# Memory read of layer 3: scores of two token tiles by seven half-size products, and rows weighted on another engine

## The chip, the core and the metric

The kernel runs on one core of a Trainium2 chip. The metric is the device time of one execution in microseconds; smaller is better. The profile names the engines PE (matrix products, TensorE), PEld (its weight loads), DVE (VectorE), ACT (ScalarE), POOL (GpSimd) and SP (SyncE, which here only issues transfers). Each engine takes its instructions strictly in the order of its own queue and waits there until what an instruction needs is ready.

## The reference, cut to what matters

The program is a chain of four layers on an image batch `x` of 4 x 512 channels x 32 x 32 positions, in 32-bit floating point. Layers 0 and 2 are attention layers, layer 1 is a gating layer. The change is nearly all in layer 3, a read of a memory of 2048 items of 512 numbers:

```python
q = jnp.transpose(x, (0, 2, 3, 1)).reshape(-1, C)   # x is group-normalized here; 4096 tokens x 512
att = q @ mempool.T                                 # 4096 x 2048 scores
vals, idx = jax.lax.top_k(att, k)                   # k = 8
vals = jax.nn.softmax(vals, axis=1)
att_sparse = jnp.zeros_like(att).at[rows, idx].set(vals)
out = att_sparse @ mempool                          # 8 weighted rows of the memory per token
```

The result is added to `x`.

## The kernel before, in words

The main path is `fast_net`; a general version of the network behind a flag is compiled in but not run on these inputs. The layers follow each other image by image (`b` from 0 to 3), with T = 1024 tokens and C = 512 channels for each image, KC = 4 blocks of P = 128 channels. In layers 0 to 2 many products of two matrices are done already by a scheme of seven half-size products (`seven`, with its sums made by `add7` and `sub7` on DVE, line 1050).

Layer 3 works on tiles of 128 tokens, 8 to an image, 32 in all (`tiles`). The normalized image is `xn3[b]`, the transposed memory is `memT`, four pieces of 128 x 2048, two of them in a buffer of their own and two in the large buffer `eT`. Nearly every instruction of this stage is put in by `pin`, so that each engine's order is the order in which the code issues them. For each tile:

- `attention` (lines 1514 to 1531) makes the 128 x 2048 scores: two halves of 1024, each in one of three PSUM places `pair` (two banks each, taken in turn by `next_pair`), each half by 8 products of 128 x 512 (line 1523), 16 products to a tile. ACT copies each half into a place `att` in SBUF (line 1528). There are three such places.
- `pick` (from line 1533) finds on DVE the eight largest scores of each token (MAX8, line 1543) and their positions (FIND_INDEX8, line 1545). POOL then issues eight indirect transfers that fetch the eight memory rows of each token into `got` (line 1548; three places). DVE makes the negated maximum (line 1554), ACT the exponentials and their sum (line 1557). SP loads the tile of `x` to be added to (line 1560).
- `read` (from line 1588) scales the weights (lines 1565 and 1566) and adds up the eight weighted rows on DVE: one product by a scalar (line 1593) and seven multiply-and-adds (line 1595). PE turns the result back to channels by tokens (line 1600) into one of two PSUM banks, `pv` and `pt`.
- `put` adds it to `x` on DVE (line 1605) and SP stores it (line 1606).

The loop at the end of `fast_net` runs over steps `s`: scores of tile s, pick of tile s-1, put of tile s-3, read of tile s-2. The last two tiles are read differently: `diagonals` (line 1572, ACT) makes diagonal matrices of the weights and `read_last` (line 1581, PE) multiplies the fetched rows by them, 32 products to a tile. Beside this, `prepare3` loads and normalizes the next image on ACT, and `behind` is a generator whose steps finish the statistics of the last image.

Just ahead of layer 3 stands the output product of layer 2's last image, `put_out2` (lines 1468 to 1488): four blocks of 16 products, each evicted by DVE in two adds, with an ACT scaling of a piece of `x` ahead of each add, and statistics behind. The scores of tile 0 stand ahead of it.

In layer 0 the gate of layer 1 is made by a generator, `gating`, whose steps ("links") are issued one at a time between other work: small products on PE, small operations on POOL, DVE and ACT. `go_on` issues the next link. At the border between two images of layer 0 `go_on` is called in each of four steps, and then once behind each product of `seven_keys` (or of `seven_by_channels` at the last border).

Of the kernel before, what the change touches and what calls it, by code (L numbers as in the profile page):

```python
# [16 lines left out]
P = 128  # L17
B = 4
# [23 lines left out]
def fast_net(ctx: ExitStack, tc: tile.TileContext, a: dict, out: bass.AP, flag: bass.AP):  # L42
# [147 lines left out]
    def tokens(src):  # L190
        return lambda k, n: src[:, k, n * NB:(n + 1) * NB]
# [56 lines left out]
    def big(tag, name):  # L248

        return apool.tile([P, KC, T], F32, tag=tag, name=name)  # L250
# [3 lines left out]
    def eight_k(shape, name, at=None):  # L254

        if at is None:
            at = turns8[0] % 3
            turns8[0] += 1
        return apool.tile(shape, F32, tag=f"w{at}", name=name)
# [1205 lines left out]
        nc.vector.tensor_mul(  # L1465
            I["o"][:, m, n * NB:(n + 1) * NB], I.pop(("pv", m, n)), I.pop(("rb", m, n)))

    def put_out2(b):
        I = img[b]
        s1 = l2[b][1]  # L1470
        mv = small.tile([P, KC, 2], F32, tag="mv", name=f"mv_d{b}")

        def add_out(m, ps):
            st = small.tile([P, 2, 6], F32, tag="bnst", name=f"st_d{b}_{m}")
            for n in range(T // NB):
                xr = apool.tile([P, NB], F32, tag="xr", bufs=2, name=f"xr_c{b}_{m}_{n}")
                nc.sync.dma_start(out=xr, in_=x1[b][:, m, n * NB:(n + 1) * NB])
                pin(nc.scalar.activation(
                    xr, xr, AF.Identity, bias=I["tb"][:, m:m + 1], scale=s1[:, m:m + 1]))
                nc.vector.tensor_add(xr, ps[:, n * NB:(n + 1) * NB], xr)  # L1480
                nc.sync.dma_start(out=x2[b][:, m, n * NB:(n + 1) * NB], in_=xr)
                nc.vector.bn_stats(st[:, n, :], xr)
            nc.vector.bn_aggr(mv[:, m, :], st.rearrange("p i s -> p (i s)"))

        for m in range(KC):
            project(I["Wp"], tokens(I["o"]), m, None, lambda ps: add_out(m, ps), f"p2_{b}")
        gc3 = const.tile([P, 2, KC], F32, tag=f"gc3_{b}", name=f"gc3_{b}")
        l3[b] = (mv, gc3)

# [21 lines left out]
            ))  # L1511
            yield

    def attention(b, tt, between=None):

        nm = f"{b}_{tt}"
        att = eight_k([P, NI], f"att_{nm}")
        for i, (lo, hi) in enumerate(
                ((0, T), (T, T + NB), (T + NB, NI)) if (b, tt) == tiles[-1] else ((0, T), (T, NI))):
            sc = flat2(next_pair())  # L1520
            for i0 in range(lo, hi, NB):
                for k in range(KC):
                    pin(nc.tensor.matmul(  # L1523
                        sc[:, i0 - lo:i0 - lo + NB],
                        xn3[b][:, k, tt * P:(tt + 1) * P], memT[k][:, i0:i0 + NB],
                        start=(k == 0), stop=(k == KC - 1),
                    ))
            pin(nc.scalar.copy(att[:, lo:hi], sc[:, 0:hi - lo]))  # L1528
            if between is not None and i == 0:
                between()  # L1530
        return att

    def pick(b, tt, att):

        nm = f"{b}_{tt}"
        top = small.tile([P, TOPK], F32, tag="top", name=f"top_{nm}")
        if (b, tt) == tiles[-1]:
            tops = small.tile([P, 3, TOPK], F32, tag="tops", bufs=1, name="tops")
            for i, (lo, hi) in enumerate(((0, T), (T, T + NB), (T + NB, NI))):
                pin(nc.vector.max(tops[:, i, :], att[:, lo:hi]))  # L1540
            pin(nc.vector.max(top, tops.rearrange("p i n -> p (i n)")))
        else:
            pin(nc.vector.max(top, att))  # L1543
        ix = small.tile([P, TOPK], mybir.dt.uint32, tag="ix", name=f"ix_{nm}")
        pin(nc.vector.max_index(ix, top, att))
        got = big("qkv"[(b * TC + tt) % 3], f"got_{nm}").rearrange("p k (i c) -> p (k i) c", c=C)
        for i in range(TOPK):
            pin(nc.gpsimd.indirect_dma_start(  # L1548
                out=got[:, i, :], out_offset=None, in_=a["mem"],
                in_offset=bass.IndirectOffsetOnAxis(ap=ix[:, i:i + 1], axis=0),  # L1550
                bounds_check=NI - 1, oob_is_err=False,
            ))
        nmx = small.tile([P, 1], F32, tag="nmx", name=f"tmx_{nm}")
        pin(nc.vector.tensor_scalar_mul(nmx, top[:, 0:1], -1.0))  # L1554
        et = small.tile([P, TOPK], F32, tag="et", name=f"et_{nm}")
        rs = small.tile([P, 1], F32, tag="rs", name=f"trs_{nm}")
        nc.scalar.activation(et, top, AF.Exp, bias=nmx, scale=1.0, accum_out=rs)
        i = (b * TC + tt) % 3
        xr = eT_flat[:, i * NB:(i + 1) * NB].rearrange("p (k q) -> p k q", q=P)
        nc.sync.dma_start(out=xr, in_=x2[b][:, :, tt * P:(tt + 1) * P])  # L1560
        return got, et, rs, xr

# [9 lines left out]
            pin(nc.scalar.activation(dg[:, i, :], ident, AF.Identity, scale=et[:, i:i + 1]))  # L1572
        return dg

    def read_last(b, tt, picked, dg):

        got, et, rs, xr = picked
        tp = next_bank().rearrange("p (k q) -> p k q", q=P)
        for i in range(TOPK):
            for m in range(KC):  # L1580
                pin(nc.tensor.matmul(
                    tp[:, m, :], got[:, i, m * P:(m + 1) * P], dg[:, i, :],
                    start=(i == 0 and m == 0), stop=(i == TOPK - 1),
                    skip_group_check=True,
                ))
        return tp, xr

    def read(b, tt, picked):
        got, et, rs, xr = picked
        nm = f"{b}_{tt}"  # L1590
        weigh(et, rs, nm)
        acc = apool.tile([P, NB], F32, tag="rb", bufs=2, name=f"acc_{nm}")
        pin(nc.vector.tensor_scalar_mul(acc, got[:, 0, :], et[:, 0:1]))
        for i in range(1, TOPK):
            pin(nc.vector.scalar_tensor_tensor(  # L1595
                acc, got[:, i, :], et[:, i:i + 1], acc, ALU.mult, ALU.add
            ))
        tp = next_bank().rearrange("p (k q) -> p k q", q=P)
        for m in range(KC):
            pin(nc.tensor.transpose(tp[:, m, :], acc[:, m * P:(m + 1) * P], ident))  # L1600
        return tp, xr

    def put(b, tt, done):
        tp, xr = done
        pin(nc.vector.tensor_add(xr, tp, xr))
        nc.sync.dma_start(out=out_v[b, :, :, tt * P:(tt + 1) * P], in_=xr)
# [136 lines left out]
    for b in range(B):  # L1743
# [18 lines left out]
        for s in range(STEPS, STEPS + LAG):  # L1762
# [14 lines left out]
            if s == STEPS + KC and not last:  # L1777
                nxt[keys[2]] = load_w(keys[2], f"{keys[2]}_n{b}", 2)
        run_out(img[b]["scale"])
        if last:  # L1780
            collect_last(b)
        load, take = statistics(b + 2) if b + 2 < B else (None, None)
# [68 lines left out]
        places7[key] = nine[3 * i:3 * i + 3]  # L1851
    places7["Wq"] = places7["Wp"]
    nc.gpsimd.tensor_scalar_mul(same, same, 8.0 / T)
    tiles = [(b, tt) for b in range(B) for tt in range(TC)]
    atts, picks, sums = {}, {}, {}
    scores2(0, UNITS2[0])
    for b in range(B):
# [29 lines left out]
            first7[2]()  # L1887
        apply2(b, UNITS2[-1])
        if last:
            atts[0] = attention(*tiles[0], lambda: invert2(b))  # L1890
            finish2(b)
            put_out2(b)
            continue
        over_keys(b, *UNITS2[-1][:2])
        at_border[0] = True
# [36 lines left out]
        nc.vector.tensor_scalar(  # L1932
            flag, tps[0:1, 0:1], float(2 * P * NS * B * (TC + 2 * KC)), None, ALU.not_equal)

    ahead, behind = iter(()), chain(behind, norm3(B - 1))
    end = len(tiles)
    diags = {}

    def pick_last(s):
        at = s - 1  # L1940
        picks[at] = pick(*tiles[at], atts.pop(at))
        put(*tiles[s - 3], sums.pop(s - 3))
        weigh(*picks[at][1:3], f"{tiles[at][0]}_{tiles[at][1]}")

    for s in range(end + 3):
        closing = end - 1 <= s <= end
        if closing:
            pick_last(s)
        if s < end:
            b, tt = tiles[s]  # L1950
            if s > 0:
                atts[s] = attention(b, tt, (lambda: diags.update(
                    {0: diagonals(0, picks[end - 2][1])})) if closing else None)
        if 0 <= s - 1 < end and not closing:
            picks[s - 1] = pick(*tiles[s - 1], atts.pop(s - 1))
        if s == end:
            diags[1] = diagonals(1, picks[end - 1][1])
        if s >= 3 and not closing:
            put(*tiles[s - 3], sums.pop(s - 3))
        if 0 <= s - 2 < end:  # L1960
            at = s - 2
            sums[at] = (read(*tiles[at], picks.pop(at)) if at < end - 2
                        else read_last(*tiles[at], picks.pop(at), diags[at - end + 2]))
        if s < end and tt == 2:
            ahead = prepare3(b + 1) if b + 1 < B else iter(())
        if s < end and tt >= 2:
            next(ahead, None)
        if s < end and 1 <= s <= TC:
            next(behind, None)
        if s == TC + 2:  # L1970
            check_range()
        if s == TC + 4:
            again = nc.values_load(flag, min_val=0, max_val=1)
    return again


# [702 lines left out]
```

## Time and profile before

| | us |
|---|---|
| median of 3 runs | 2510.26 (2508.2 to 2510.97) |
| profiled execution, its own time | 2512.0 |
| its span, first to last instruction | 2510.3 |
| PE busy | 2470.4 (98%) |
| DVE busy | 1820.5 (73%) |
| ACT busy | 1023.3 (41%) |
| POOL busy | 1225.5 (49%) |
| scores of tile 1 begin | 2047.29 |
| scores of tile 31 issued, transposes of tile 29 begin (timeline) | 2486.26 |
| last add (line 1605) begins | 2505.01 |

In the page each group of instructions is one line: line of the source, engine, operation, result and operands, shape and count, then busy time in microseconds, mean duration of one in nanoseconds, and the idle time of the engine just ahead of it with what ended that. A product of 32-bit numbers shows as two records in the trace, so 16 products of 128 x 512 are 32 records. The ends of matrix products are modelled by the profiler.

Rows of the page that the change touches, other than those quoted below:

```profile
L1548 POOL DMA_INDIRECT got<-in_mem,ix x256 | 277.7, 1085 | 214.9 <-DVE tmx L1554 146.2 <-issue 63.7 <-DMA got<-in_mem,ix 4.6
L1528 ACT COPY att<-pair 128x1024 f32<-128x1024 f32 (+1 forms) x65 | 64.9, 999 | 217.3 <-PE pair L1523 217.2
```

The first is the 256 indirect transfers of POOL (8 for each tile), the second ACT's copies of the scores; ACT mostly waits for PE there.

### The profile page before, as it was taken

The numbers are of one execution on the slowest core, as the hardware profiler recorded it, in microseconds if no ns is written. First come the engines' busy times: TensorE is split into PE (matmuls) and PEld (weight loads), VectorE is DVE, ScalarE is ACT, GpSimd is POOL, SyncE is SP. The second block draws the span as 40 slices with busy tenths as digits, with TensorE's granted clock in tenths as the row PEclk, the third lists the DMA queues.
The fourth block names the chain that finished last, engine by engine and source line by source line (L and its number), as shares of the span: only waits on it lengthen the run. The fifth ranks groups of instructions, "written<-read, shape, count | busy, mean of one in ns | idle before, by whom it ended". The sixth has DMA issues, their size and how long they took to land.

```text
span 2510.3 us, 48081 instructions
## 1 busy us (share of the span) xinstructions
PE 2470.4 (98%) x18512; PEld 1173.5 (47%) x18512; DVE 1820.5 (73%) x2962; ACT 1023.3 (41%) x1246; POOL 1225.5 (49%) x1688
## 2 busy tenths in 40 slices
PE   9999999999999999999999999999999999999998
PEld 4344534555355534555633633453363344444445
DVE  5799568875788548886768677576757647888876
ACT  1567346652666336651253145125314512121212
POOL 3266415553455426554274247127405617565665
PEclk9999999999999999999999999999999999999999
DMA  2588348882698538893301230230113146667666
GB/s 85 160 227 229 111 135 220 241 220 85 174 245 232 139 89 210 245 245 128 109 18 68 105 126 18 64 125 31 55 50 135 31 133 191 214 191 217 185 189 177
DMA packets 190031, 367.19 MB, mean 146 GB/s; under 512 B 32985, under 2 KB 96473, under 8 KB 185570
## 3 DMA queue, kind: packets, MB, share of 16 engines
q1 hardware_dynamic: 109712, 186.58, 24.1%
q0 software_dynamic: 49152, 142.79, 21.0%
q10 hardware_dynamic: 30930, 34.66, 5.2%
q8 instruction: 149, 2.44, 0.4%
q14 instruction: 88, 0.72, 0.1%
HBM read 190.10 MB, written 39.58 MB: 91 GB/s over the span
## 4 chain that ended last, share of the span: by engine, by line
PE 87%; DVE 5%; DMA 3%; ACT 2%; issue 1%; POOL 1%; SPq 0%; ACTq 0%; POOLq 0%
PE pair L1523 18%; PE pair L1123 13%; PE pv L578 8%; PE pair L1371 8%; PE pair L513 6%; PE pair L199 6%; PE pair L539 5%; PE pt L471 5%; PE pt L1408 4%; PE pv L1408 4%; PE pair L1249 4%; PE pt L767 4%; DMA s<-ss 2%; ACT e L546 2%; DVE out L1050 1%
## 5 line engine op out<-in xcount | busy, mean ns | idle before, releaser
L528 POOL DMA_DIRECT2D s<-ss x512 | 258.1, 512 | 394.9 <-issue 115.0
L552 DVE STREAM_TRANSPOSE eT<-e 128x1024 f32<-128x1024 f32 x256 | 316.6, 1237 | 185.1 <-ACT e L546 184.5
L1548 POOL DMA_INDIRECT got<-in_mem,ix x256 | 277.7, 1085 | 214.9 <-DVE tmx L1554 146.2
L1365 ACT ACTIVATE eT<-pair 128x1024 f32<-128x1024 f32 x256 | 248.2, 1022 | 312.4 <-PE pair L1371 188.8
L567 DVE BATCH_NORM_STATS2 st<-e 128x6 f32<-128x256 f32 x1024 | 350.8, 405 | 0.0
L1389 POOL TENSOR_TENSOR e<-eT 128x1024 f32<-128x1024 f32 x96 | 239.4, 2497 | 166.9 <-ACT eT L1365 122.5
L546 ACT ACTIVATE e<-pair 128x1024 f32<-128x1024 f32 x256 | 250.7, 1022 | 165.4 <-PE pair L539 129.4
L519 ACT COPY ss<-pair 128x1024 f32<-128x1024 f32 x256 | 247.1, 1018 | 87.0 <-PE pair L513 43.0
L513 PE MATMUL pair<-k,q 64*32 64x512 f32 x4096 | 267.3, 598 | 11.7 <-ACT e L546 11.7
L578 PEld LDWEIGHTS pv<-eT,v 128*64 128x64 f32 x4096 | 221.1, 137 | 71.9 <-issue 55.2
L578 PE MATMUL pv<-eT,v 128*64 128x128 f32 x4096 | 250.0, 275 | 4.3 <-ACT pv L638 4.3
L1371 PE MATMUL pair<-q,k 64*128 64x512 f32 x1024 | 239.9, 605 | 1.8 <-DVE sum L1050 0.9
L1390 DVE TENSOR_TENSOR eT<-eT,e 128x1024 f32<-128x1024 f32 x96 | 144.7, 1507 | 129.1 <-POOL e L1389 128.9
L539 PE MATMUL pair<-s,wmix 32*32 32x512 f32 x4096 | 161.1, 600 | 4.8 <-DMA s<-ss 3.8
L1595 DVE SCALAR_TENSOR_TENSOR acc<-got,et,acc 128x512 f32<-128x512 f32 x210 | 157.9, 752 | 7.5
L1385 POOL TENSOR_TENSOR eT<-eT 128x1024 f32<-128x1024 f32 x32 | 83.4, 2606 | 156.1 <-ACT eT L1365 151.2
L1371 PEld LDWEIGHTS pair<-q,k 64*128 64x128 f32 x1024 | 92.3, 186 | 140.0 <-issue 66.6
L1528 ACT COPY att<-pair 128x1024 f32<-128x1024 f32 (+1 forms) x65 | 64.9, 999 | 217.3 <-PE pair L1523 217.2
L513 PEld LDWEIGHTS pair<-k,q 64*32 64x32 f32 x4096 | 57.0, 105 | 177.4 <-ACT e L546 85.8
L1050 DVE TENSOR_TENSOR k<-k,pair 128x512 f32<-128x512 f32 (+1 forms) x96 | 78.1, 858 | 64.9 <-PE pair L1123 51.2
L1543 DVE MAX8 top<-att 128x8 f32<-128x2048 f32 x31 | 71.1, 2293 | 72.4 <-ACT att L1528 72.4
L651 POOL TENSOR_TENSOR o<-pv,rb 64x256 f32<-64x256 f32 x128 | 118.8, 928 | 6.2
(384 smaller groups left out, 3748.0 us busy)
## 6 DMA issues: line engine op xcount, KB each, us to landing
s<-ss SPq DMA_DIRECT2D x512, 128.0 KB
s<-ss POOLq DMA_DIRECT2D x512, 128.0 KB, 4.6
rb<-r POOLq DMA_DIRECT2D x64, 128.0 KB, 6.1
o<-o SPq DMA_DIRECT2D x32, 256.0 KB
xr_c<-x SPq DMA_DIRECT2D x32, 256.0 KB
rb_c<-r SPq DMA_DIRECT2D x64, 128.0 KB
eT<-x SPq DMA_DIRECT2D x32, 256.0 KB
out<-eT SPq DMA_DIRECT2D x32, 256.0 KB
```

Source lines behind the costliest of these rows:

```text
L513: pin(nc.tensor.matmul(sc[m * NS:(m + 1) * NS, r, :], q[r * HD:(r + 1) * HD, m, s * NS:(s + 1) * NS], k_[r * HD:(r + 1) * HD, m, n * NB:(n ...
L528: pin(relays[side].dma_start(out=s2[2 * m + r::NH], in_=ss[m * NS:(m + 1) * NS, r, :]))
L539: pin(nc.tensor.matmul(mixed(s, r // 2)[t * NS:(t + 1) * NS, r % 2, :].rearrange("p (qq k) -> p qq k", qq=2), wmix[r * NS:(r + 1) * NS], s ...
L546: pin(nc.scalar.activation(e[:, half].rearrange("p r qq k -> p (r qq k)"), flat2(mixed(s, half)), AF.Exp))
L552: pin(nc.vector.transpose(eT[:, j % 2].rearrange("p b (qq i r) x -> p i r qq b x", qq=2, i=4)[:, i, 2 * half:2 * half + 2], e[:, half].rea ...
L567: pin(nc.vector.bn_stats(st[:, i, 2 * half + r, qq, :], e[:, half, r, qq, :]))
L578: pin(nc.tensor.matmul(pv[r * HD:(r + 1) * HD, gp, :], I["v"][:, t, g * HD:(g + 1) * HD], eT[:, j % 2, t, :, 4 * g:4 * g + 4], start=(t == ...
L1123: pin(nc.tensor.matmul(ps[:, m, :], w[:, k, m * P:(m + 1) * P], x[:, k, :], start=(k == 0), stop=(k == 1)))
L1365: pin(nc.scalar.activation(e, scs[len(es)], AF.Exp, scale=SCALE))
L1371: pin(nc.tensor.matmul(sc[:, r, :], I["k"][r * HD:(r + 1) * HD, m, t * P:(t + 1) * P], I["q"][r * HD:(r + 1) * HD, m, n * NB:(n + 1) * NB] ...
L1523: pin(nc.tensor.matmul(sc[:, i0 - lo:i0 - lo + NB], xn3[b][:, k, tt * P:(tt + 1) * P], memT[k][:, i0:i0 + NB], start=(k == 0), stop=(k == ...
L1548: pin(nc.gpsimd.indirect_dma_start(out=got[:, i, :], out_offset=None, in_=a["mem"], in_offset=bass.IndirectOffsetOnAxis(ap=ix[:, i:i + 1], ...
```

## The change

**Scores of two tiles together.** `tiles` is reordered so that tiles n and n+1 (n even) are token blocks t+4 and t of one image. For 14 of the 16 pairs (n = 2 to 28) `two_tiles` makes both tiles' scores by seven products of half size instead of eight: [128 tokens x 256 channels] times [256 channels x 1024 items], 4 products of 128 x 512 each, 28 in place of 32 for a pair. It needs sums on both sides. Those of the memory are made once, on DVE, by `memory_sums`: eight operations of 128 x 1024, two behind each block of `put_out2`, kept in the first 8192 columns of `eT`. Those of the tokens are made on DVE for each pair: `token_sums` makes s3, s1, s2 at the end of the pair before, and s4 is made at the pair's start; each is 128 x 256. The seven products, here P1 to P7 in their order, go into three PSUM places: x takes P1, P3, P5 and P7 and is never cleared in between, z takes P2 and P4, y takes P6. ACT copies x behind P1, z behind P2, x behind P3 and x behind P7 into the score places; DVE adds z behind P4, x behind P5 and y (P6) onto them. The first two and the last two tiles still go through `attention`.

**Weighting and adding of rows.** In place of the chain of line 1593 and 1595, `ready` makes the reciprocal on DVE and scales the weights on ACT; `weigh_rows` multiplies each of the eight fetched rows by its weight on ACT, in place (128 x 512 each, in two pieces of four); `add_up` adds the eight rows on DVE by three adds of 128 x 1024 and one of 128 x 512. The transposes (`turn_back`) and `put` follow later, one pair behind, in pieces spread over the pair.

**Order.** All of it is written out by hand. For a pair n the queue of DVE is, in order: s4; add_up of tile n-4; MAX8, FIND_INDEX8 and negated maximum of tile n-1; reciprocal of n-2; add_up of n-3; add of z (P4); put of n-4; add of x (P5); reciprocal of n-1; MAX8, FIND_INDEX8 and negated maximum of tile n; add of y (P6); s3, s1, s2 of the next pair; put of n-3. The queue of ACT is: four rows of n-3; copy behind P1; four rows of n-3; exponentials of n-1; copy behind P2; copy behind P3; scaling of n-2; four rows of n-2; scaling of n-1; four rows of n-2; exponentials of n; copy behind P7. On PE the transposes of n-4 stand behind P2 and those of n-3 behind P5. The places of `x` tiles move from `eT` to four places in `e`. The closing steps for tiles 26 to 31 are written out; the last two tiles still use `diagonals` and `read_last`.

**A gate link ahead of k.** One more `go_on()` is called at each border of layer 0, ahead of the seven products that make k.

```diff
-    def put_out2(b):
+    def put_out2(b, between):
...
             project(I["Wp"], tokens(I["o"]), m, None, lambda ps: add_out(m, ps), f"p2_{b}")
+            next(between)
...
+    def memory_sums():
+
+        def raw(h, i):
+            return [memT[2 * h + k][:, i * T:(i + 1) * T] for k in range(2)]
+
+        t1, t2, t3, t4 = ([t[:, k, :] for k in range(2)] for t in mem_t)
+        for out, x, y in ((t1, raw(0, 1), raw(0, 0)), (t2, raw(1, 1), t1),
+                          (t3, raw(1, 1), raw(0, 1)), (t4, raw(1, 0), t2)):
+            for part in zip(out, x, y):
+                sub7(*part)
+            yield
...
+    def token_sums(n):
+
+        a11, a12, a21, a22 = token_blocks(n)
+        s1, s2, s3, s4 = token_places
+        sub7(s3, a11, a21)
+        add7(s1, a21, a22)
+        sub7(s2, s1, a11)
+
+    def two_tiles(n):
...
+        x, z, y = (next_pair() for _ in range(3))
+        next_pair()
+        sub7(s4, a12, s2)
...
+        for ps, start, a_, b_, use, to in (
+                (x, True, a11, raw(0, 0), "=", one[:, left]),
+                (z, True, s3, of(2), "=", other[:, right]),
+                (x, False, s2, of(1), "=", other[:, left]),
+                (z, False, a22, of(3), "+", other[:, left]),
+                (x, False, s1, of(0), "+", other[:, right]),
+                (y, True, a12, raw(1, 0), "+", one[:, left]),
+                (x, False, s4, raw(1, 1), "=", one[:, right])):
+            for c in range(2):
+                for k in range(2):
+                    pin(nc.tensor.matmul(
+                        ps[:, c, :], a_[:, k, :], b_(k, c),
+                        start=(start and k == 0), stop=(k == 1), skip_group_check=True))
+            if use == "=":
+                pin(nc.scalar.copy(to, flat2(ps)))
+            elif ps is not y:
+                add7(to, to, flat2(ps))
+            yield other
+            if ps is y:
+                last = lambda: add7(one[:, left], one[:, left], flat2(y))
+        last()
+        yield one
...
-    def read(b, tt, picked):
...
-        weigh(et, rs, nm)
-        acc = apool.tile([P, NB], F32, tag="rb", bufs=2, name=f"acc_{nm}")
-        pin(nc.vector.tensor_scalar_mul(acc, got[:, 0, :], et[:, 0:1]))
-        for i in range(1, TOPK):
-            pin(nc.vector.scalar_tensor_tensor(
-                acc, got[:, i, :], et[:, i:i + 1], acc, ALU.mult, ALU.add
-            ))
+    def ready(n, picked):
+
+        got, et, rs, xr = picked
+        ri = small.tile([P, 1], F32, tag="ri", name=f"tri_{n}")
+        pin(nc.vector.reciprocal(ri, rs))
+        pin(nc.scalar.activation(et, et, AF.Identity, scale=ri))
+
+    def weigh_rows(picked, lo, hi):
+        got, et, rs, xr = picked
+        for i in range(lo, hi):
+            pin(nc.scalar.activation(
+                got[:, i, :], got[:, i, :], AF.Identity, scale=et[:, i:i + 1]))
+
+    def add_up(n, picked):
+        got, et, rs, xr = picked
+        acc = apool.tile([P, NB], F32, tag="rb", bufs=2, name=f"acc_{n}")
+        for to, of in ((0, 2), (4, 6), (0, 4)):
+            add7(got[:, to:to + 2, :], got[:, to:to + 2, :], got[:, of:of + 2, :])
+        add7(acc, got[:, 0, :], got[:, 1, :])
+        return acc, xr
...
         run_out(img[b]["scale"])
+        go_on()
...
+    for n in range(2, end - 2, 2):
+        b, j = tiles[n][0], n // 2 % (TC // 2)
+        parts = two_tiles(n)
+
+        if n > 2:
+            weigh_rows(picks[n - 3], 0, 4)
+        next(parts)
+        if n > 2:
+            weigh_rows(picks[n - 3], 4, TOPK)
+            add_tile(n - 4)
+        picks[n - 1] = pick(n - 1, atts.pop(n - 1))
...
+        next(parts)
+        if n > 2:
+            turn_tile(n - 4)
+
+        next(parts)
...
+        ready(n - 2, picks[n - 2])
+        if n > 2:
+            add_tile(n - 3)
+
+        next(parts)
+        if n > 2:
+            put_tile(n - 4)
+        weigh_rows(picks[n - 2], 0, 4)
...
+        atts[n] = next(parts)
+        if n > 2:
+            turn_tile(n - 3)
+        ready(n - 1, picks[n - 1])
+        weigh_rows(picks[n - 2], 4, TOPK)
+
+        next(parts)
...
+        picks[n] = pick(n, atts.pop(n))
+
+        next(parts)
+        atts[n + 1] = next(parts)
+        if n + 2 < end - 2:
+            token_sums(n + 2)
+        if n > 2:
+            put_tile(n - 3)
...
+    s = end
+    picks[s - 1] = pick(s - 1, atts.pop(s - 1))
+    turn_tile(s - 4)
+    weigh(*picks[s - 1][1:3], s - 1)
+    add_tile(s - 3)
+    put_tile(s - 4)
+    turn_tile(s - 3)
+    diags[1] = diagonals(1, picks[s - 1][1])
+    put_tile(s - 3)
+    sums[s - 2] = read_last(picks.pop(s - 2), diags[0])
+    sums[s - 1] = read_last(picks.pop(s - 1), diags[1])
+    put_tile(s - 2)
+    put_tile(s - 1)
```

In the loop, `next(parts)` issues the next of the seven products with its copy or add, and the steps between these calls are what the order above lists.

## The prediction, made before the changed kernel was run

> **What bounds the kernel now.** I read the chain that ended last first. In layer 3 it is PE and nothing else:
>
> ```profile
> 2160.24 0.44 PE pt L1600 x4
> 2160.68 13.73 PE pair L1523 x32
> 2174.41 0.44 PE pv L1600 x4
> 2174.85 13.74 PE pair L1523 x32
> ...
> 2486.86 7.16 PE pv L1581 x64
> ...
> 2502.06 2.93 PE pt L1581 x24
> 2505.01 0.69 DVE eT L1605
> ```
>
> Columns: start, length, what. A tile costs 13.73 us of scores (16 products, 0.858 each) and 0.44 of transposes, 14.17 us, without a gap from tile to tile until 2486; then a tail in which the last tiles are read. The table by stretches, for 114 us of this stage, says how full the others are:
>
> ```profile
> 2294.00:2408.00 114.00, 114.00 (x291) 52.02 (x290) 92.23 (x123) 24.14 (x38) 70.19 (x65) 1.00 0.64 185
> ```
>
> PE 114.00 of 114, DVE 92.23 (81%), ACT 24.14, POOL 70.19, clock 1.00. So four products fewer for a pair are 3.43 us off the bound, if DVE, the next, allows it. Its costs come from the groups kept apart by shape and from the timeline:
>
> ```profile
> L1595 DVE SCALAR_TENSOR_TENSOR acc<-got,et,acc 128x512 f32<-128x512 f32 x210 | 157.9, 752 | 7.5
> L1050 DVE TENSOR_TENSOR v<-v,pair 128x1024 f32<-128x1024 f32 x32 | 38.3, 1217 | 6.9 <-PE pair L1249 6.9
> L1050 DVE TENSOR_TENSOR eT<-eT 128x1024 f32<-128x1024 f32 x6 | 7.3, 1219 | 0.0
> L1050 DVE TENSOR_TENSOR eT<-eT 128x256 f32<-128x256 f32 x20 | 7.1, 423 | 0.0
> ```
> ```profile
> 2161.32 2.29 DVE L1543 MAX8 top<-att 128x8 f32<-128x2048 f32 x1 [2.46 <-ACT att L1528]
> ...
> 2163.65 0.09 DVE L1545 MATCH_VALUE_LOAD ix<-top,att 128x8 f32 x1
> 2163.73 2.29 DVE L1545 FIND_INDEX8 ix<-top,att 128x8 uint32<-128x2048 f32 x1
> 2165.93 0.14 DVE L1554 TENSOR_SCALAR tmx<-top 128x1 f32<-128x1 f32 x1
> 2165.98 0.68 DVE L1605 TENSOR_TENSOR eT<-pt,eT 128x512 f32<-128x512 f32 x1
> 2166.10 0.30 ACT L1557 ACTIVATE et<-top,tmx 128x8 f32<-128x8 f32 x1 [4.81 <-DVE tmx L1554]
> ...
> 2166.31 0.18 ACT L1557 ACTIVATION_READ_ACCUMULATOR et<-top,tmx 128x1 f32 x1
> ```
>
> The starts matter. A DVE instruction that needs nothing of the one before it starts 0.08 before that one's end (2163.73 to 2165.93, 2.20 for a 2.29); one that needs its result starts 0.035 after it (MAX8 to the load of its values, 2.33 for 2.29). Below, "step" is start to start. ACT takes the exponentials 0.04 after the negated maximum ends.
>
> **The change, part by part.** PE for a pair: 28 x 0.858 + 0.88 = 24.9 us, against 2 x 14.17 = 28.34.
>
> DVE for a pair, in steps: two picks (2.33 + 0.08 + 2.20 + 0.05 each) 9.3; three adds from PSUM (1.217 long) 3.5; four token sums (0.423 long, two followed by one that needs them) 1.5; two tiles of row adds (1.14 + 1.25 + 1.25 + 0.60) 8.5; two puts 1.2; two reciprocals 0.2. Together 24.2, 97% of PE's 24.9. There is hardly room for DVE to wait, and it does wait: for P4 and P5. So I follow one loop instead of adding sums.
>
> The wait that the change adds: ACT's exponentials of tile n-1 stand ahead of the copies behind P2 and P3, and need DVE's pick of n-1. Queued behind them is the copy of z, and P4 adds into z, so PE waits. And P5 is what DVE's pick of tile n needs. From the end of P5 to the end of the next pair's P5: add of x 1.25, with the wake-up 1.29; pick of n to the negated maximum 4.61; that 0.05; add of y 1.13; s3, s1, s2, put, s4 0.34 + 0.46 + 0.34 + 0.60 + 0.34 = 2.08; row adds of n-4 4.24; pick of n-1 to the end of the negated maximum and ACT's start 4.78; exponentials 0.30; copy 1.01 and PE's wake-up 0.13 (as from the landing at 2501.93 to the product at 2502.06) 1.14; P4 and P5 6.86 and the last product's own end 0.17. Sum 26.65 us. PE then stands 1.75 us in each pair ahead of P4.
>
> Nothing else is late: ACT needs about 16 us a pair, its rows are done 4 us ahead of the exponentials; POOL's 16 fetches at 1.37 (1.085 and the gaps between) are 21.9 of 26.65, and a row fetched has over 4 us from landing to its weighting; x's adds behind P5 end 2 us ahead of P7.
>
> The first pair has no tile to add up and takes about 24.0. So 14 pairs take 24.0 + 13 x 26.65 = 370.5 in place of 28 x 14.17 = 396.8: 26.3 us saved, not the 48 of the products (56 x 0.858).
>
> Weighting on ACT against a rule of the Trainium skill, "ScalarE: Activation LUTs", Rules for kernel authors: multiply belongs on VectorE, not on ScalarE. The row for DVE is L1593, 0.494 long (0.41 a step). For ACT no row has this shape: 128 x 128 with the same kind of scale took 0.389 (L1572), and 0.81 is a 128 x 512 with a bias as well (L1478); I take 0.71, a step of 0.61, the lower one scaled by size. By the rule 16 rows would put 6.6 us on DVE, make its pair 30.8 and the kernel slower than now; by the rows ACT's 9.8 (11.4 at the upper end) lie beside DVE's work at no cost. The rows decide.
>
> Memory sums: 8 x 1.22 = 9.8 us of DVE beside put_out2. A block of that is 6.87 us of PE with 2.9 of DVE, and 2.4 more fit; behind the last block they push the pick of tile 0 by 2.4, which nobody waits for until P2 of the first pair. Cost 0; without that cover up to 2.4.
>
> The tail gets longer. Now the last transposes end at 2486.86, the diagonal products of tile 30 follow at once, and those of tile 31 end at 2505 with the last fetch. After the change the transposes of tile 29 stand ahead of the diagonal products, and wait for DVE. Counted from the end of the scores: negated maximum at 4.2 as now; its exponentials on ACT behind the last copy, four rows (4 x 0.61) and eight diagonals (8 x 0.29), at 5.4; reciprocal and weights to 6.3; row adds of 29 to 10.6; transposes and put of 28 to 11.3; then 7.16 for tile 30 and 7.16 for tile 31, whose rows have all landed by 17.5 (last fetch issued at 2499.91, 3.9 to landing); last add at about 25.8. Now it is 2505.01 - 2486.26 (where the timeline has the last transposes begin) = 18.75. Cost 7.1 (5 to 8.5).
>
> The gate link: PE stands 0.74 us twice ahead of L968, for ACT's copy out of the shared bank. The link moved up ends that, but the product of v behind it must wait for DVE's copy of the gate, 0.2 to 0.5, three times. Bounds -1.5 to +1; I take -0.5.
>
> Sum: -26.3 + 7.1 - 0.5 = -19.7. The profiled execution took 2512.0, 1.7 over its span and 1.7 over the median of 2510.26; taken from the median, 2490.6, rounded to 2491.
>
> **Rivals.** *PE stays without gaps.* If DVE's steps overlap better than I read, only PE's 24.9 counts: 14 x 3.43 - 7.1 + 0.5 = 41.5 saved, about 2469. For it: DVE's sum is below 24.9. Against: the loop alone is 26.65, each term from a row.
>
> *Slower: the new adds are held by POOL's fetches.* The Trainium skill, "GPSIMD Engine Reference", Key points, says that POOL shares its SBUF interfaces with DVE and contends with DVE instructions that have two SBUF inputs. All row adds and token sums are of that kind, and fetches will fill 82% of the pair. Where POOL ran such additions itself, DVE's L1390 adds of 128 x 1024 went from 1.22 to as much as 3.38, mean 1.507. At half as long again for each of these adds (4.34 and 4 x 0.42 in the loop, +3.0), a pair takes 29.65, 14 of them 12.6 more than now, the tail some 10: about 2532. It decides from 27.85 a pair, where the gain just pays for the tail: +1.2 us. Against it stands L1595, also with two SBUF inputs, beside the same fetches: 0.750 to 0.773 in 210 instructions. The trace contradicts the rule for fetches, so I give it little.
>
> *Part of it:* small added waits (a PE restart of 0.3, adds 5% longer) bring a pair to 27.2 to 27.6: 2498 to 2506.
>
> **Chances.** 2491 with its own range 2483 to 2499: 0.70. Gapless: 0.07. Part: 0.14. Held adds: 0.09. The range 2479 to 2506 leaves out the gapless end and the slower case. Faster by over 0.2% (5.0 us, about what a measurement can tell): 0.84; within: 0.07; slower: 0.09.
>
> **What would show it.** In the profile after: pairs 26.65 apart, with PE idle 1.5 to 2 us once a pair ahead of the product into z, ended by ACT's copy; ACT idle at the exponentials for DVE's negated maximum; DVE over 88% busy; row adds 1.22 long; ACT rows 0.71; clock at 1.00; the last add about 25.8 behind the last score product. It is wrong if the row adds are longer than 1.3, if PE waits at P2, P3 or P7 too, or if the diagonal products begin less than 8 us behind the scores.

## The result and the profile after

The changed kernel takes 2505.11 us (median of 22 runs, 2501.11 to 2512.93) against 2510.99 for the kernel before (22 runs): ratio 0.998, 95% interval 0.9972 to 0.9988, 5.9 us less. The prediction said 19.7 less and a range that ends at 2506. The sign was right; less than a third of the gain came. That 2505 still lies inside the wide range is no success: the range gave its upper end to longer pairs, and those did not come, as shown below.

The execution that was profiled took 2504.67 us, its span is 2503.0 (before: 2512.0 and 2510.3). The two spans, cut at the same events:

| part | before | after | change | predicted |
|---|---|---|---|---|
| start of the scores of the second tile | 2047.13 | 2044.64 | -2.5 | -0.5 |
| from there to the end of the scores | 439.30 | 417.60 | -21.7 | -26.3 |
| from there to the start of the last add | 18.6 | 33.85 | +15.3 | +7.1 |
| from there to the end | 5.3 | 6.9 | +1.6 | 0 |

(The prediction counted the tail before from the last transposes, 18.75.) So the pairs gave a little less than forecast, and the tail took twice what was forecast.

The table by stretches of the profile after, for the 114 us that were shown of before (columns: stretch, its length, PE, PEld, DVE, ACT, POOL with the number of instructions, granted clock, DMA share, GB/s):

```profile
2294.00:2408.00 114.00, 107.80 (x274) 48.52 (x273) 103.66 (x118) 68.50 (x116) 71.18 (x68) 1.00 0.70 196
```

PE now stands 6.2 us in this stretch, where it had no gap; DVE is 91% busy, and ACT went from 24 to 68. Where PE stands is seen in the timeline of one pair (start, length, what, and in brackets the idle time before and what ended it):

```profile
2337.76 0.13 DVE L1631 TENSOR_SCALAR tmx<-top 128x1 f32<-128x1 f32 x1
...
2337.93 0.30 ACT L1634 ACTIVATE et<-top,tmx 128x8 f32<-128x8 f32 x1 [4.01 <-issue]
...
2338.23 1.91 ACT L1600 COPY att<-pair 128x1024 f32<-128x1024 f32 x2
2339.27 3.27 PE L1596 MATMUL pair<-eT,xn_d 128*128 128x512 f32 x7 [1.55 <-ACT att L1600]
```

It is the loop of the prediction, step for step: DVE's negated maximum, ACT's exponentials, the copy of z, the product into z. (The profile names no releaser for the exponentials' wait of 4.01 us; they start 0.04 us behind the end of the maximum, like those in the prediction's lines.) These gaps follow each other at 2284.26, 2311.00, 2337.72, 2364.45: 26.73 us a pair, against 26.65 worked out. The groups of DVE and ACT in the pairs, apart by shape (busy time, mean ns of one, idle before):

```profile
L1050 DVE TENSOR_TENSOR got<-got 128x1024 f32<-128x1024 f32 x81 | 97.2, 1229 | 0.9
```
```profile
L1674 ACT ACTIVATE got<-got,et 128x512 f32<-128x512 f32 x216 | 138.0, 711 | 1.3 <-DMA got<-in_mem,ix 1.0
```

The row adds take 1.229 us beside POOL's fetches, against 1.219 for the same shape before, so the rival of the held adds is out. ACT's rows take 0.711, the estimate was 0.71. The chain that ended last shows the tail:

```profile
2455.37 6.87 PE pair L1531 x16
2462.24 2.78 issue
2465.03 1.69 PE pv L1689 x4
...
2478.72 1.11 PE pt L1689 x4
2479.83 9.07 PE pv L1657 x64
2488.90 7.16 PE pt L1657 x64
2496.06 0.02 issue
2496.09 0.69 DVE e L1695
```

(L1531 are the last scores, L1689 the transposes, L1657 the diagonal products of tiles 30 and 31, L1695 the last add.) The diagonal products of tile 30 begin 17.6 us behind the scores; the prediction had 11.3. They take 9.07 us, those of tile 31 take 7.16: the same 64 instructions.

### The profile page after: what moved, and what is told of

It is laid out like the page before. It is cut to its first block, busy times and chain, and to the rows that moved or that the text cites. A ratio compares the mean times of both kernels' runs of the same rounds, so it can differ in the third digit from the quotient of the medians.

```text
span 2503.0 us, 47967 instructions
## 1 busy us (share of the span) xinstructions
PE 2430.2 (97%) x18400; PEld 1154.5 (46%) x18400; DVE 1847.7 (74%) x2918; ACT 1175.1 (47%) x1516; POOL 1215.8 (49%) x1688
## 5 line engine op out<-in xcount | busy, mean ns | idle before, releaser
L1596 PE MATMUL pair<-eT,tokens 128*128 128x512 f32 x448 | 201.3, 592 | 0.0
L1674 ACT ACTIVATE got<-got,et 128x512 f32<-128x512 f32 x240 | 153.2, 711 | 1.4 <-DMA got<-in_mem,ix 1.0
L1596 PEld LDWEIGHTS pair<-eT,tokens 128*128 128x128 f32 x448 | 84.1, 190 | 100.9 <-issue 98.1
```

What stands on the lines that cost most here:

```text
L1596: pin(nc.tensor.matmul(ps[:, c, :], a_[:, k, :], b_(k, c), start=(start and k == 0), stop=(k == 1), skip_group_check=True))
```

## The experiments

Fifteen runs. They did not all run on the same chip: the first four ran on one chip, the next four on a second, three more on that second one, and the last four on a third; each is compared with runs of the kernel before on its own chip (medians 2511.14, 2511.25, 2509.19 and 2510.02). It turned out that this matters. The record does not name the chip of the result above; its profile looks like those of the first chip.

**Another order of the last tiles.** On PE the diagonal products of tile 30 ahead of the transposes of tile 29, and the queues of ACT and DVE to match:

```diff
     def second_part():
         turn_tile(s - 4)
-        weigh_rows(picks[s - 2], 0, 4)
+        weigh(*picks[s - 1][1:3], s - 1)
+        diags[0] = diagonals(0, picks[s - 1][1])
+        weigh_rows(picks[s - 2], 0, 4)
...
+    add_tile(s - 3)
     put_tile(s - 4)
-    weigh(*picks[s - 1][1:3], s - 1)
-    add_tile(s - 3)
+    turn_tile(s - 3)
     weigh_rows(picks[s - 2], 4, TOPK)
-    diags[0] = diagonals(0, picks[s - 1][1])
+    sums[s - 1] = read_last(picks.pop(s - 1), diags[0])
...
     turn_tile(s - 3)
...
-    sums[s - 2] = read_last(picks.pop(s - 2), diags[0])
     sums[s - 1] = read_last(picks.pop(s - 1), diags[1])
```

> The changed kernel with another order of its last two tiles and nothing else. On PE the diagonal products of tile 30 come ahead of the transposes of tile 29; on ACT the diagonals of tile 30 come ahead of the rows of tile 29, which are weighted around the copies of tile 31; on DVE the row adds of tile 28 come ahead of the put of tile 27, and the pick of tile 31 ahead of the row adds of tile 29. Theory 'the tail's order': what was lost behind the scores is lost because tile 30's products stand in queues behind tiles 28 and 29, so the last add comes 19 to 21 us behind the end of the scores in place of 34, the clock keeps its full rate there, and the time is 12 to 15 us below the changed kernel's 2505 (ratio to the kernel before 0.992 to 0.993). Rival 'late ends on PE': the put of tile 27 and the two last copies waited 4 to 8 us longer than the products they need, for a reason that is not their place in a queue; then that comes back here, the last add stays 26 us or more behind the scores, and the gain is 3 to 7 us. The pairs stay at 26.73 us.

Measured: 2495.05 us, ratio 0.9944 (0.9926 to 0.9963), 10 us below the changed kernel. The last add comes 27.3 us behind the scores, in place of 34. That is between the two theories: the order costs, and the copies of tile 31 were late here too, by 5.1 and 6.0 us.

**The exponentials behind the copies.** `pick` hands back the call of the exponentials of tile n-1, and it is made behind the copies of the second and third product:

```diff
-        picks[n - 1] = pick(n - 1, atts.pop(n - 1))
+        held_back = []
+        picks[n - 1] = pick(n - 1, atts.pop(n - 1), held_back)
...
         next(parts)
+        held_back.pop()()
         next(behind, None)
```

> The changed kernel with one instruction moved: in each pair, ACT's exponentials of the tile before stand behind the copies of the second and third product and no longer ahead of them. Theory 'the loop': PE's 1.55 us ahead of the product into z end, the pair is then bound by DVE's own sum and PE's 24.9 and takes 25.0 to 25.6 us in place of 26.73; over 13 pairs that is 15 to 22 us, ratio to the kernel before 0.989 to 0.992. Rival 'DVE alone sets 26.7': DVE was 93% busy, and the exponentials only happen to stand there; then the gap moves to another product and the pair stays above 26.3, at most 5 us gained. The tail stays 34 us long, as in the changed kernel.

Measured: 2478.13 us, ratio 0.9873 (0.9854 to 0.9892), 27 us below the changed kernel: more than expected. The table by stretches of this run:

```profile
2294.00:2408.00 114.00, 114.00 (x293) 52.14 (x292) 109.99 (x124) 72.25 (x122) 78.62 (x74) 1.00 0.73 209
```

PE has no gap, DVE is 96% busy, and in the pairs the chain that ended last is PE alone. One pair of it (L1596 are the scores, L1693 the transposes):

```profile
2314.12 10.30 PE pair L1596 x24
2324.42 0.44 PE pt L1693 x4
2324.86 13.74 PE pair L1596 x32
2338.59 0.44 PE pv L1693 x4
```

That is 24.92 us a pair, PE's own sum. One instruction's place in ACT's queue was worth 1.81 us in each of 13 pairs, 23.5; the rest is the next run's subject, which a PE without gaps absorbs as well (one gap of 0.42 is left).

**The flag's load in the first pair.**

```diff
+    check_range()
     token_sums(2)
...
-        if n == 12:
-            check_range()
-        if n == 14:
+        if n == 2:
             again = nc.values_load(flag, min_val=0, max_val=1)
```

> The changed kernel with the range check ahead of the first pair and the load of its flag in the first pair, in place of pairs 6 and 7. Theory 'the load lets the order slip': two pairs of the changed kernel took 28.70 and 28.42 us in place of 26.73, since around the flag's load the row adds of one tile got mixed with the pick of another, PE then stood 2.88 us and its clock was granted at half for 3.4 us, 1.7 us of products. Without it all periods are 26.7, no half clock is left inside the stage, and 3.6 us are gained against the changed kernel (ratio to the kernel before 0.996 to 0.997). Rival: something else of those two pairs (the loads of the next image's tokens, ACT's scaling of them, which stand there too) costs it; then the two long periods stay at pairs 6 and 7 and nothing is gained.

Measured: 2502.23 us, ratio 0.9969 (0.9957 to 0.998). From the second tile's start to the end of the scores it takes 414.12 us where the changed kernel took 417.60: 3.5 us, as expected, and all 13 gaps are 1.43 to 1.59 us. The edit moves the range check with the load, so the two are not told apart by it; what happened at the load is in the changed kernel's timeline of DVE:

```profile
2223.55 2.28 DVE L1620 MAX8 top<-att 128x8 f32<-128x2048 f32 x1
2225.76 1.20 DVE L1050 TENSOR_TENSOR got<-got 128x1024 f32<-128x1024 f32 x1
2226.88 0.08 DVE L1622 MATCH_VALUE_LOAD ix<-top,att 128x8 f32 x1
2226.95 2.28 DVE L1622 FIND_INDEX8 ix<-top,att 128x8 uint32<-128x2048 f32 x1
```

A row add of tile 11 stands between the maximum and the index of tile 13, and another add of tile 11 stood ahead of the maximum; in every other pair these adds follow the pick. As written, both adds stand behind the pick, so across the load the order as written did not hold. The pick came 2 us late, and then PE was slow as well (changed kernel, table by stretches):

```profile
2223.00:2231.00 8.00, 4.69 (x14) 2.13 (x14) 7.96 (x8) 5.82 (x10) 4.92 (x5) 1.00 0.78 268
2231.00:2235.00 4.00, 4.00 (x6) 1.52 (x5) 0.14 (x1) 0.52 (x1) 3.09 (x4) 0.57 0.54 140
```

Behind a gap of 2.88 us the granted clock is 0.57 over 4 us (half from 2231.15 to 2234.57), so 3.41 us of products were done at half rate: 1.7 us more.

**Without the gate link.**

```diff
         run_out(img[b]["scale"])
-        go_on()
```

> The changed kernel without the gate link moved up. Prediction's step: 0.5 us slower than the changed kernel. Rival: the 2.5 us by which layer 3 began earlier in the profile after (2002.9 against 2005.4) are the link's, and come back: 2.5 us slower, with PE's two stops of 0.77 us ahead of the gate's product back at about 622 and 907 us. The tail is the changed kernel's own, so this is also a second look at it: if the put of tile 27 again starts about 4 us behind its transposes and the copy of tile 31's third quarter about 8 us behind its products, that delay belongs to the program, and if not, to that one execution.

Measured: 2505.92 us, ratio 0.998 (0.9973 to 0.9987), 0.8 us above the changed kernel, within what can be told from nothing. PE's two stops of 0.77 us are back, at 618.17 and 902.27. Layer 3 did not begin later (1998.31). In fourteen profiles of kernels that have the link it began between 1998.84 and 2005.65: the 2.5 us of the table above are within this scatter between executions. The tail was late again: the last add 34.25 us behind the scores.

**Useless products behind the last scores.** Eight products are added whose result nobody reads, on PE behind the scores of tile 31:

```diff
     atts[s] = attention(s, second_part, (att_at[0] + 2) % 3)
+    idle = flat2(next_pair())
+    for i0 in range(0, T, NB):
+        for k in range(KC):
+            pin(nc.tensor.matmul(
+                idle[:, i0:i0 + NB], xn3[B - 1][:, k, 0:P], memT[k][:, i0:i0 + NB],
+                start=(k == 0), stop=(k == KC - 1)))
```

> The changed kernel with eight score products more (6.86 us of PE) behind those of tile 31, written into a free pair of banks that nobody reads; order and waits of everything else are unchanged. In all four profiles with the new tail, the put of tile 27 and the two last copies of tile 31's scores began 1 to 8 us behind the end of the PE work that they need, while elsewhere such a start comes 0.03 us behind it; in each, the next thing in PE's queue was a wait (for DVE's row adds, or for a fetch). Theory 'PE standing in a wait reports late': with PE still fed, those copies start within 0.1 us of their products, the exponentials of tile 31 come about 5 us earlier, and although PE does 6.86 us of useless work the last add comes 26 to 29 us behind the useful scores in place of 34, which is 4 to 7 us below the changed kernel. Rival 'late for another reason' (a DMA's traffic, the program's place): the copies stay 5 us or more late and the time stays or grows by up to 4 us.

Measured: 2497.35 us, ratio 0.9953 (0.9936 to 0.997). The starts were at once (0.02 to 0.04 us behind their products), the last add 27.2 us behind the useful scores. The theory seemed shown. It was not: this run was on another chip.

**The three edits together, and with the useless products.**

> The three edits together: the tail's order, ACT's exponentials behind the copies, the flag's load in the first pair. If they are independent, the gains of the single runs add: 10.1 + 27.0 + 2.9 below the changed kernel, about 2465 us (ratio to the kernel before 0.982). If the shorter pairs leave tiles 28 to 30 later against the end of the scores, the tail gives some back: up to 2473. Pairs at 24.9 without a gap on PE.

Measured: 2466.8 us, ratio 0.983 (0.9814 to 0.9847); pairs of 24.9 us, last add 21.6 us behind the scores. That this is near the expected 2465 is luck. On this chip the changed kernel itself takes 2497.89 (the control below), so the three edits bring 31 us and not 40. Two things were counted too high. The move of the exponentials and the early load are not independent: from the second tile's start to the end of the scores it takes 390.80 us here, and 391.44 with the exponentials moved alone. And the tail gains 5.8 us against the control's 27.4, where 10.1 had been put down to it.

> The three edits together and the eight useless products behind tile 31's scores. If PE standing in a wait reports late, tile 31's copies come 5 us earlier, its fetches too, and the last add with them: 3 to 5 us below the run with the three edits alone. If not, it stays the same, or is up to 3 us longer where the useless products hold tile 30's diagonal products up.

Measured: 2467.73 us, ratio 0.9836 (0.9819 to 0.9853): no gain.

**The rows weighted by DVE**, `nc.vector.tensor_scalar_mul` in place of ACT's instruction:

> The changed kernel with the rows weighted by DVE in place of ACT, all 30 tiles of them. Prediction's reasoning: sixteen rows at 0.41 us a step are 6.6 us more DVE in a pair; DVE is on the loop, so a pair takes 33.3 us in place of 26.7, 13 pairs lose 86 us, and the kernel is about 2590, slower than before. Rival (the rule that multiplication belongs on VectorE): DVE's rows are short and ACT's 9.8 us a pair were what made the loop late; the pair then stays under 28 us and the kernel under 2525.

Measured: 2570.52 us (one run). Most pairs take 31.4 us, near the 30.8 that the prediction had for DVE's sum, with DVE busy for 30.4 of them; the expected 33.3 put the rows on top of the loop of 26.7, but PE's gap, 4.1 us, now stands ahead of the transposes, where it waits for DVE's row adds. Against the changed kernel on the same chip (2497.89) this run is 73 us longer: the rule for multiplications that the prediction sets aside would have lost here.

**The changed kernel again, beside the useless products elsewhere.** The first is the unaltered kernel. In the second the eight products stand behind the transposes of tile 28, in the third there are four of them ahead of these transposes.

> The changed kernel itself, unaltered, beside the two below on one chip. The run with the useless products, in which tile 31's copies began at once, ran on another chip than the runs in which they were late; so the chip may be the cause and not the products. Theory 'PE's queue': here the put of tile 27 starts 1 us or more behind its transposes and the copies of tile 31 5 us or more behind their products, as in the profile after; about 2505. Rival 'the chip': all within 0.1 us, the last add 26 to 28 us behind the scores, about 2497.

> The changed kernel with the eight useless products behind the transposes of tile 28, in place of ahead of them: PE's queue first meets the wait for DVE's row adds of tile 28, as in the changed kernel, and is fed only after it. Theory 'a wait at the head of PE's queue makes the ends before it late': the put of tile 27 and the copies are as late as in the control until tile 28's adds are done, time within 3 us of the control. Theory 'PE kept busy': the copies of tile 31 are late, but those ends that fall in the useless products come at once. Rival 'the chip': no start late here either, about 2497.

> The changed kernel with four useless products (3.43 us) ahead of the transposes of tile 28 in place of eight. Theory 'PE's queue': the starts are at once, as with eight, and the time is 4 to 8 us below the control on the same chip. Rival 'the chip': no difference to the control beyond 2 us in when these copies start.

Measured: 2497.89 (ratio 0.9958, 0.9947 to 0.9968), 2497.7 (0.9951, 0.9928 to 0.9973) and 2497.78 (0.9949, 0.9932 to 0.9967). The unaltered kernel has no late start either on this chip. The useless products do nothing here, wherever they stand: the run that seemed to show the theory of PE's queue shows nothing of it, and of the two 'the chip' is left. The timeline of ACT in the control:

```profile
2457.18 0.59 ACT L1536 COPY att<-pair 128x512 f32<-128x512 f32 x1 [0.36 <-PE pair L1531]
2460.61 0.59 ACT L1536 COPY att<-pair 128x512 f32<-128x512 f32 x1 [2.85 <-PE pair L1531]
```

and the same two copies in the profile after, whose products ended at 2458.81 and 2462.24:

```profile
2466.74 0.59 ACT L1536 COPY att<-pair 128x512 f32<-128x512 f32 x1 [8.27 <-PE pv L1689]
2468.22 0.58 ACT L1536 COPY att<-pair 128x512 f32<-128x512 f32 x1 [0.89 <-remote]
```

In the control they start 0.04 us behind the products, in the profile after 7.9 and 6.0; there the put of tile 27 was 4.2 late as well. On a third chip:

> The changed kernel, unaltered, to tell which sort of chip this is: last add 27.4 us behind the scores and about 2498 where nothing is late, 34 us and about 2505 where the put of tile 27 and the last copies start late.

> The changed kernel with the eight useless products behind tile 31's. If the control is late: theory 'engines that stand waiting' expects these starts at once and some 7 us below the control; theory 'the chip' expects them late here too and the time within 3 us of the control. If the control is not late: within 3 us of it, as on the earlier chip.

> The three edits together. Where nothing is late: 2467, last add 21.6 us behind the scores. If the control is late and it goes with the chip: the last add 26 to 29 us behind, about 2472 to 2474.

> The kernel before, for its tail on this chip: the copies of its last tile 0.2 us behind their products and the last add 18.7 us behind the scores where nothing is late. If the chip makes every end of PE late in a tail, its copies are late as well and the last add comes 21 us behind or later.

Measured: the changed kernel 2494.8 (ratio 0.9938, 0.9916 to 0.9961), no start late, last add 27.4 us behind the scores; with the useless products 2498.56 (0.996, 0.9942 to 0.9977); the three edits 2461.07 (0.9801, 0.9773 to 0.983), last add 20.8; the kernel before 2512.33 (one run), its last copy 0.04 us behind its products. So this chip is of the second sort too, and what the products would do where starts are late was not seen. The kernel before takes the same on all three (2511.14; 2511.25 and 2509.19; 2510.02): the late starts cost time in the new tail only.

## Why the prediction was wrong

**The loop: right.** 26.73 us a pair for 26.65, the gap of 1.55 at the place and with the releaser that were named, DVE 91% busy. That ACT's exponentials are the cause is shown: their move takes the gap away and gives 24.92, the 24.9 of PE's sum. The rival of PE without gaps described the kernel that one moved instruction makes.

**The pairs' sum: 4.6 us short.** "14 pairs take 24.0 + 13 x 26.65" took all pairs as equal. 13 times 0.08 is 1.0; the two pairs at the flag's load took 28.70 and 28.42 in place of 26.73, 3.7. I had left the load and the check out of the working, since they were in the kernel before. There DVE had 19% to spare; here nothing covered them.

**The tail: this is the step that failed.** "Cost 7.1 (5 to 8.5)": in the profile after it was 15.3. The control says how much was the step's own. In its chain:

```profile
2465.98 0.29 ACT et L1634 x2
...
2470.32 0.75 DVE acc L1050
...
2472.23 8.56 PE pv L1657 x64
2480.79 7.16 PE pt L1657 x64
```

With its scores ended at 2460.57, the exponentials start at 5.4 (predicted 5.4), the row adds end at 10.5 (10.6), the products of tile 30 start at 11.7 (11.3), and the last add stands at 27.4 (25.8). The queues were read right. What was mis-sized is the diagonal products of tile 30: 8.56 us for 7.16. PE had stood 10.11 us, and its clock was at half from 2464.82 to 2475.06, so over the first part of these products (table by stretches of the control):

```profile
2472.23:2475.06 2.83, 2.83 (x15) 2.83 (x15) 0.69 (x1) 0.00 (x0) 2.22 (x3) 0.50 0.87 238
```

Half of these 2.83 us is the missing 1.4. The Trainium skill, "TensorE: Matmul & The Clock Gate", Part 1, says that an idle window of about 3.4 us halves the clock; I had a wait of some 10 us in my own working and did not charge it. With 27.4 less 18.6 the tail costs 8.8 us in the control, over the 8.5 that the range allowed. The rest, 33.85 less 27.40, 6.5 us, goes with the late starts (0.5 of it is a longer stretch at half clock), which nothing in the profile before announced. For the tail the prediction's sign of being wrong was diagonal products that begin too early, under 8 us; it set none for too late.

**The rest.** The gate link's 0.8 us can't be told from nothing, as small as forecast. The end behind the last add took 6.9 us in this execution and 5.3 to 7.0 in others. One sum of the prediction is off without bearing on the result: the pair at which the gain just pays for the tail was worked out for 14 equal pairs (27.85); with its own first pair of 24.0 it is 28.1.

The shortfall of the profiled execution, 12.4 us, is then: tail 8.2 (6.5 late starts, 1.4 clock, 0.3 waits), pairs 4.6, end 1.6, less 2.0 by an earlier start. On the two other chips the same kernel gains 11 and 15 us (2497.89 and 2494.8), inside 2483 to 2499: there the forecast of 2491 is too low by 4 to 7, most of it the flag's load (3.7) and the half clock (1.4).

What stays open is what makes an engine start 1 to 9 us behind PE's end on one chip; since the profiler models that end, PE itself may have been late. It was seen in the profile after and in the four experiments of the first chip, and in none of the ten profiles of the new tail on the two others; since the unaltered kernel starts promptly there, useless products are not needed for it. Whether they help on the first chip wasn't tried. Nor was that chip measured again in a second session: that the late starts go with the chip, and not with the session, is not shown.

## What to carry to other kernels

When an engine fills up, go back over what already stood on it: a check, a load of a flag, an order that was slack before becomes a loss, and the order in which the engine ran them shows it. Ahead of a copy that PE waits for, nothing should stand in ACT's queue that waits for another engine: here one moved instruction brought 27 us, and the three edits 31 to 34 against the changed kernel on the same chips. And a control belongs beside an experiment, on its chip: without it the useless products would have passed as a cure.

## What was not expected of the hardware

PE's stop at the flag's load (2.88 to 3.31 us) went with its clock at half for 3.41 or 6.83 us in each of the nine profiles that have it, and so did each of the 13 stops of 4.0 to 6.1 us in the run with the rows on DVE. The stops of 1.4 to 1.6 in the pairs never did, nor did the 2.46 us in the tail of before. So a stop shorter than the 3.4 us of the Trainium skill ("TensorE: Matmul & The Clock Gate", Part 1) can be enough. Its length alone does not decide: in the run with four useless products, 1.99 us in layer 0 (at 1104.2) were followed by 3.41 us at half. In the profile after, a gap of 13.04 us went with 17.07 us at half.

On the first chip, and in the profile after, engines that waited for PE beside and behind the last scores started 1 to 9 us later than PE's instructions ended, while in the pairs before, and on the two other chips in the tail too, they started within 0.11 us.
